# Splitting the softmax terms, placing the statistics' steps and reloading z in a dilated-attention kernel

## The chip, the cores and the metric

The kernel runs on one core of a Trainium2 chip. The metric is device microseconds of one execution. Five runs of the kernel before gave 5422.48 to 5433.66 us, with a median of 5424.08 us.

The engines are named as the profile names them: PE (TensorE) with PEld for its weight loads, DVE (VectorE), ACT (ScalarE), POOL (GpSimd) and SP (SyncE, whose queue issues nearly all DMAs).

## The reference

The input x is 16 images of 56 x 56 pixels and 384 channels, in float32. Two layers are computed, each of them a residual on a group norm with 32 groups of 12 channels:

```
x = x + attention(group_norm(x), w_qkv, w_proj, b_proj)
x = x + depthwise_conv3x3(group_norm(x), sign(clip(w, -1, 1)))
```

The attention is local. The 384 channels of q, k and v are three groups of 128 with dilations 1, 2 and 3, each of 4 heads of 32 channels. A pixel attends to its 9 neighbours in a 3 x 3 pattern with that dilation; outside the image k and v are zero:

```
scores  = sum over 32 channels of q[pixel] * k[neighbour], times 32 ** -0.5
weights = softmax over the 9 neighbours
out     = sum over 9 neighbours of weights * v[neighbour]
y       = out, three groups side by side, times w_proj, plus b_proj
```

The statistics of a group norm cover a whole image, so each layer of an image can start only when the layer before it has finished the image.

## The kernel before, in words

**Tiling.** An image is cut into 7 chunks of 8 rows (448 pixels), so there are 112 chunks. Channels lie on the partitions, pixels along the free dimension. Three stages run through the chunks in a software pipeline, all at the same time on different chunks:

- `plan_a` loads x, transposes it on PE (`turn`, L412), copies it out on ACT, collects statistics on DVE (L425), and writes it to DRAM as `xd`.
- `plan_b` is the attention. `load_x` and `normalise` prepare `xn`; `k_or_v` and `query` project it on PE (L463); `score` multiplies q by k on DVE (L516) and sums over channels on PE (L501); `softmax_1` to `softmax_3` make the weights; `turn_weights` (L566) transposes them with a DMA from SP into `aT`; `weigh` spreads them over the channels on PE (L579), multiplies by v on DVE (L586, into a buffer `w` of a pool of three) and adds on POOL (L594, L597, L598); `out_project` multiplies by w_proj on PE (L612), adds the residual on DVE (L615), collects statistics (L618) and writes `x1d` to DRAM (L620).
- `plan_c` is the convolution. Two thirds of the channels go through PE: `load` (L688) brings `z`, three shifted copies of the rows with 32 channels each, `normalise` scales it on ACT (L701) and sets edges to zero on POOL (L682, L703), `convolve` (L715) multiplies by diagonal matrices, and DVE adds the residual (L722). The last third (`xg`, L729, normalised into `zg` at L740) is scaled by its nine taps on ACT (L762) and added on POOL (L768, L773, L776). `turn` transposes the result back (L783), ACT copies it (L785), and it is written out (L788).

In the last image, where no attention runs any more beside the convolution, `plan_c` takes other ways: the nine taps of `xg` run on DVE (`taps_last`, L753), one z set of four is normalised on DVE (L697), outputs are issued from ACT, and z is loaded as `z_last` into pairs of sets in buffers that the attention has left (pool `t` for even chunks, pool `w` and one `xn` for odd ones). Each pair takes three transfers, one for each of the three rows of taps (`ky`).

**The softmax weights.** The weights are made in float32 (`ew`) and then written as three bfloat16 terms whose sum is the weight. ACT casts the first term (L558), POOL subtracts it (L559, into `rest`), ACT casts the second (L560), POOL subtracts again and so makes the third (L561). All four stand in `softmax_3`.

**The statistics.** `group_norm` makes six steps: `channels` aggregates on DVE (L305); `mean`, `deviation` and `variance` each sum over groups with small matmuls (L311, L321, L331); `invert` computes an inverse square root with 13 small instructions on POOL (L345 to L349); `spread_out` copies mean and scale back to the channels with small matmuls (L354 into `pp`, and L367 into `pz` for the convolution) and two copies on DVE (L358 `mr`, L372 `mrz`). For the input of the convolution all later work on an image (`zg`, `z`) needs `mr` or `mrz`.

**What sets the order.** The function `at(when, order, piece)` files each piece of work under a slice and an order inside the slice; a chunk advances by 9 slices (`STEP`). The pieces are issued sorted by slice and order. This is a priority, not yet the queue: when the program is built, a planner walks through a model of the machine and lets each engine take, of the instructions whose inputs and buffers it expects to be ready, the one of the highest priority. The result is one fixed queue for each engine, which the chip runs in order; an instruction that waits holds up all that stand behind it. DMAs stand in the queue of the engine that issues them. The orders of a slice are

```
SOFTMAX, SCORE, CONVOLVE, WEIGH, QUERY, STATISTICS, QKV, PROJECT, STAGE_A, STAGE_C, NORM, LOADS
```

The six steps of the statistics of `x1` are filed at slices 0, 1, 2, 4, 5 and 7 after the image's last `out_project` (`STAT1_SLICE`), those of x likewise (`STAT0_SLICE`), all of them with order `STATISTICS`.

Of the kernel before, what the change touches and what calls it, by code (L numbers as in the profile page):

```python
# [8 lines left out]
F32 = mybir.dt.float32  # L9
# [3 lines left out]
ALU = mybir.AluOpType  # L13
# [4 lines left out]
P = 128  # L18
HEADS = 4
HD = 32  # L20
NG = 3
NTAP = 9
NQ = 4
ROWS = 8
SUB = 112
# [3 lines left out]
NPAD = 32  # L29
K_SLOTS, V_SLOTS = 2, 3  # L30
RSQRT_BITS = 0x5F3759DF
TERMS = 3
# [3 lines left out]
def dilated_attention_then_binary_conv(  # L36
# [28 lines left out]
    nc = tc.nc  # L65
# [214 lines left out]
    def rows(ap):  # L280
        return ap.rearrange("p (r w) -> p r w", w=W)
# [100 lines left out]
    def at(when, order, piece):  # L382

        pieces.setdefault((when, order), []).append(piece)
# [6 lines left out]
    def plan_a(m, t0):  # L391
# [41 lines left out]
        def norm(k):  # L433
            if k == 0:
                steps["of"] = group_norm(stats0.pop(b), lambda mr: mr0.update({b: mr}))
            steps["of"][k]()
# [3 lines left out]
            at(t0 + 2 * j if b else FIRST + 2 * c + 1, STAGE_A, lambda j=j: turn(j))  # L440
        if c == NCH - 1:
            for k in range(6):
                at(t0 + 5 + STAT0_SLICE[k], STATISTICS, lambda k=k: norm(k))

    def plan_b(m, t0):

# [98 lines left out]
        def softmax_2():  # L545
# [2 lines left out]
            nc.vector.reciprocal(sm, sm)  # L548
            nc.vector.tensor_tensor(by_neighbour(weights), by_neighbour(weights), over_neighbours(sm), ALU.mult)

        def softmax_3():

            rest = s_p.tile([SUB, NSUB * NPAD * HEADS], F32, tag="rest", name="rest")
            eights = "p (u k) -> p u k"
            e8 = ew.rearrange(eights, k=8)
            r8 = rest.rearrange(eights, k=8)
            term = [e3.rearrange("p s u (r k) -> p (s u r) k", r=4)[:, :, 8 * t : 8 * t + 8] for t in range(TERMS)]
            nc.scalar.copy(term[0], e8)  # L558
            nc.gpsimd.tensor_tensor(r8, e8, term[0], ALU.subtract)  # L559
            nc.scalar.copy(term[1], r8)  # L560
            nc.gpsimd.tensor_tensor(term[2], r8, term[1], ALU.subtract)  # L561

# [61 lines left out]
        def norm(k):  # L624
            if k == 0:
                steps["of"] = group_norm(stats1.pop(b), lambda mr, mrz: mr1.update({b: (mr, mrz)}), True)
            steps["of"][k]()
# [10 lines left out]
        at(t0 + 9, SOFTMAX, softmax_1)  # L638
        at(t0 + 10, SOFTMAX, softmax_2)
        at(t0 + 11, SOFTMAX, softmax_3)  # L640
        at(t0 + 12, LOADS, turn_weights)
        for i in range(9):
            at(t0 + 14 + i, WEIGH, lambda i=i: weigh(i))
# [2 lines left out]
            at(t0 + 24 + j, PROJECT, lambda j=j: out_project(j))  # L646
        if c == NCH - 1:
            for k in range(6):
                at(t0 + 27 + STAT1_SLICE[k], STATISTICS, lambda k=k: norm(k))

    def plan_c(m, t0):

# [16 lines left out]
        def load(j):  # L669
            by_set = x1d[b].rearrange("(j q c) n -> j c q n", q=NQ, c=HD)[j]  # L670
            if b < B - 1:
                z = z_p.tile([P, NQ * PX], F32, tag="z", name="z")[:K3].rearrange("p (q n) -> p q n", q=NQ)
                had[f"z{j}"] = [(z, 0, NQ)]
            else:

                had[f"z{j}"] = []
                for q0 in range(0, NQ, 2):
                    pool, tag = (t_p, "t") if c % 2 == 0 else (w_p, "w") if (j, q0) != (1, 2) else (xn_p, "xn")
                    z = pool.tile([P, 3, PX], F32, tag=tag, name="z_last")[:K3, :2]
                    had[f"z{j}"].append((z, q0, q0 + 2))  # L680
            for edge in edges(j):
                nc.gpsimd.memset(edge, 0.0)  # L682
            for ky in range(3):
                lo = W if c == 0 and ky == 0 else 0
                hi = PX - W if c == NCH - 1 and ky == 2 else PX
                n0 = p0 + (ky - 1) * W
                for z, q0, q1 in had[f"z{j}"]:
                    nc.sync.dma_start(  # L688
                        z[ky * HD : (ky + 1) * HD, :, lo:hi], by_set[:, q0:q1, n0 + lo : n0 + hi]
                    )  # L690

        def normalise(j):
            mrz = mr1[b][1]
# [31 lines left out]
        zp = zg[m % 2]  # L725

        def load_g():
            had["xg"] = xg = xg_p.tile([P, ROWS + 2, W], F32, tag="xg", name="xg")
            nc.sync.dma_start(  # L729
                xg[:, lo:hi, :].rearrange("p r w -> p (r w)"),  # L730
                x1d[b][JG * P : (JG + 1) * P, p0 + (lo - 1) * W : p0 + (hi - 1) * W],
            )
# [57 lines left out]
        if b == B - 1:  # L790

            at(t0 - 6, LOADS, load_g)
            at(t0 - 6, LOADS, load_x)
            ahead = 3 if c else 1
            at(t0 - ahead, NORM, normalise_g)
            for j in range(JG):
                at(t0 - 5 + j, LOADS, lambda j=j: load(j))
                at(t0 - ahead + j, NORM, lambda j=j: normalise(j))
                at(t0 + 1 + j, CONVOLVE, lambda j=j: convolve(j))
            for ky in range(3):  # L800
                at(t0 + 1 + ky, CONVOLVE, lambda ky=ky: taps_last(ky))
            for s in range(NSUB):
                at(t0 + 12, STAGE_C, lambda s=s: turn(s))
            return
# [11 lines left out]
        for s in range(NSUB):  # L816
            at(t0 + 9 + s, STAGE_C, lambda s=s: turn(s))

    SOFTMAX, SCORE, CONVOLVE, WEIGH, QUERY, STATISTICS, QKV, PROJECT, STAGE_A, STAGE_C, NORM, LOADS = range(12)
    STEP = 9  # L820
    STAT0_SLICE = (0, 1, 2, 4, 5, 7)
    STAT1_SLICE = (0, 1, 2, 4, 5, 7)
    FIRST = -200
    at(FIRST, LOADS, load_weights)
    for cc in range(NG):
# [41 lines left out]
```

## Time and profile before

| what | value |
|---|---|
| median of 5 runs | 5424.08 us |
| the profiled execution's own time | 5424.08 us |
| its span, first to last instruction | 5422.4 us |
| granted clock of PE, mean | 0.978 |
| PE busy | 5206.4 us |
| POOL busy | 4219.4 us |
| DVE busy | 4141.3 us |
| ACT busy | 2401.1 us |
| HBM read and written | 466.41 MB and 231.21 MB |

Busy time is the union of an engine's instructions; a busy PE also contains time at half clock. A window of the profile lists, for each engine, the busy microseconds and the number of instructions in a stretch of the span, then the granted clock, the mean busy share of the 16 DMA engines, and GB/s. A list of waits names the engine and line that stood still, after the arrow what ended the wait, and then the total in us, the number of times and the longest. A line of the timeline has the start and the duration in us, the engine, the line of the kernel, the instruction, what it writes and reads, and in brackets how long the engine stood idle before it and what ended that. "SPq" is the DMA queue of SP.

The steady part of the program lasts from about 480 us to 4800 us. After 5262 us the attention is over and only the convolution of the last image is left.

### The profile page before, as it was taken

How to read it: one execution, taken by the hardware profiler on the slowest of the kernel's cores; microseconds unless marked ns; L12 is line 12 of the kernel's file. 1: busy time of each engine (PE TensorE's matmuls, PEld its weight loads, DVE VectorE, ACT ScalarE, POOL GpSimd, SP SyncE). 2: the span in 40 equal slices, each digit the busy share in tenths (PEclk: the TensorE clock that was granted, in tenths of full speed). 3: DMA queues.
4: the chain of work that ended last, by engine and by line, in shares of the span. 5: the costliest groups of instructions: out<-in, count | busy, mean ns of one | idle time of the engine just before them, and what ended most of it. 6: DMA issues, size and time to landing. Idle time of an engine off the chain costs nothing. (4 is left out here: it accounts for less than half of the span.)

```text
span 5422.4 us, 77496 instructions
## 1 busy us (share of the span) xinstructions
PE 5206.4 (96%) x27669; PEld 2427.8 (45%) x27669; DVE 4141.3 (76%) x4209; ACT 2401.1 (44%) x4189; POOL 4219.4 (78%) x3049
## 2 busy tenths in 40 slices
PE   8999999999999999999999999999999999999965
PEld 4444444444444444444444444444444444444422
DVE  4887778877777787777878777787777877777753
ACT  3224444445444444444445444444444445444433
POOL 2677888878888887888878888887888878888870
PEclk9999999999999999999999999999999999999976
DMA  5444555655556555555655555555555655544444
GB/s 167 126 119 125 160 158 150 161 158 161 154 157 165 163 156 161 159 157 150 165 156 161 155 156 164 162 156 162 158 157 151 166 155 162 152 136 132 129 122 129
DMA packets 811640, 825.75 MB, mean 152 GB/s; under 512 B 360307, under 2 KB 801014, under 8 KB 811254
## 3 DMA queue, kind: packets, MB, share of 16 engines
q1 hardware_dynamic: 803270, 808.79, 54.3%
q10 hardware_dynamic: 7984, 12.00, 0.7%
q8 instruction: 219, 3.59, 0.3%
q14 instruction: 167, 1.37, 0.1%
HBM read 466.41 MB, written 231.21 MB: 129 GB/s over the span
## 5 line engine op out<-in xcount | busy, mean ns | idle before, releaser
L594 POOL TENSOR_TENSOR w<-w 128x1344 f32<-128x1344 f32 x672 | 2050.6, 3051 | 459.8 <-DVE w L586 358.3
L586 DVE TENSOR_TENSOR w<-pb_a,v 128x1344 f32<-128x1344 f32 x1008 | 1560.6, 1548 | 249.5 <-PE pb_a L579 152.5
L516 DVE TENSOR_TENSOR t<-pq,k 128x1344 f32<-128x1344 f32 x1008 | 1535.3, 1551 | 245.9 <-PE pq L463 245.9
L463 PE MATMUL pkv<-xn,wqkvT 128*128 128x448 f32 x3924 | 1565.6, 548 | 0.0
L463 PEld LDWEIGHTS pkv<-xn,wqkvT 128*128 128x128 f32 x3924 | 717.3, 190 | 660.0 <-issue 629.8
L612 PE MATMUL po<-y,wprojT 128*128 128x448 f32 x2016 | 831.8, 549 | 22.4 <-POOL y L598 19.2
L768 POOL TENSOR_TENSOR m<-m 128x1344 f32<-128x1344 f32 x210 | 640.2, 3049 | 269.4 <-ACT m L762 269.4
L463 PE MATMUL pq<-xn,wqkvT 128*128 128x448 f32 x1962 | 826.7, 557 | 0.0
L701 ACT ACTIVATE z<-z,mrz 96x448 f32<-96x448 f32 x840 | 578.4, 751 | 437.9 <-DMA z<-x1d 411.2
L501 PE MATMUL ps<-t,sel 128*32 128x448 f32 x6048 | 676.9, 558 | 35.9 <-DVE t L516 35.3
L762 ACT ACTIVATE m<-zg,ktap 128x448 f32<-128x448 f32 x945 | 554.0, 658 | 285.6 <-POOL m L768 278.5
L612 PEld LDWEIGHTS po<-y,wprojT 128*128 128x128 f32 x2016 | 375.4, 191 | 375.6 <-issue 342.0
L715 PE MATMUL pc<-z,kdiag 96*32 96x440 f32 (+1 forms) x5040 | 523.0, 549 | 6.3 <-POOL z L703 4.4
L722 DVE TENSOR_TENSOR x<-pc,x 128x448 f32<-128x448 f32 x224 | 139.8, 624 | 457.5 <-PE pc L715 457.5
L463 PEld LDWEIGHTS pq<-xn,wqkvT 128*128 128x128 f32 x1962 | 345.2, 189 | 311.5 <-issue 311.5
L579 PE MATMUL pb_a<-aT,spread 24*128 24x448 bf16 x3024 | 368.7, 359 | 44.4 <-DVE w L586 39.0
L598 POOL TENSOR_TENSOR y<-y,w 128x448 f32<-128x448 f32 x336 | 381.8, 1136 | 22.6
L597 POOL TENSOR_TENSOR y<-w 128x448 f32<-128x448 f32 x336 | 382.4, 1138 | 14.7
L473 ACT COPY v<-pkv 128x448 f32<-128x448 f32 x336 | 178.8, 532 | 473.3 <-PE pkv L463 458.1
L615 DVE SCALAR_TENSOR_TENSOR xr<-po,bias,xr 128x448 f32<-128x448 f32 x336 | 227.7, 678 | 187.3 <-PE po L612 183.4
L473 ACT COPY k<-pkv 128x448 f32<-128x448 f32 x336 | 178.5, 531 | 369.5 <-PE pkv L463 369.5
L501 PEld LDWEIGHTS ps<-t,sel 128*32 128x32 f32 x6048 | 171.7, 110 | 378.7 <-issue 249.1
(128 smaller groups left out, 4406.3 us busy)
## 6 DMA issues: line engine op xcount, KB each, us to landing
z<-x1d SPq DMA_DIRECT2D x570, 224.0 KB, 4.1
xr<-xd SPq DMA_DIRECT2D x112, 672.0 KB, 4.3
x1d<-xr SPq DMA_DIRECT2D x112, 672.0 KB, 3.2
xn<-xd SPq DMA_DIRECT2D x109, 672.0 KB, 4.6
xin<-in_x_dram SPq DMA_DIRECT2D x108, 672.0 KB, 7.1
xd<-xa SPq DMA_DIRECT2D x315, 224.0 KB, 3.6
out_dram<-osb SPq DMA_DIRECT2D x420, 168.0 KB, 3.5
x<-x1d SPq DMA_DIRECT2D x112, 448.0 KB, 7.6
```

The lines of the kernel that those rows point to most:

```text
L463: nc.tensor.matmul(dst[:, :PX], wqkvT[:, cc, o0 : o0 + P], had["xn"][:, cc, :], start=(cc == 0), stop=(cc == NG - 1))
L501: return nc.tensor.matmul(had["ps"][32 * j : 32 * j + 32, :PX], sel[:, s0 : s0 + 32], tk, start=(issued[j] == 1), stop=(issued[j] == len(r ...
L516: nc.vector.tensor_tensor(t.rearrange("p k (r w) -> p k r w", w=W), q3, k3, ALU.mult)
L586: nc.vector.tensor_tensor(w.rearrange("p k (r w) -> p k r w", w=W), pb[:, :, :PX].rearrange("p k (r w) -> p k r w", w=W), three(kv[1][g][m ...
L594: nc.gpsimd.tensor_tensor(w0, w0, w, ALU.add)
L597: nc.gpsimd.tensor_tensor(y, w0[:, 0], w0[:, 1], ALU.add)
L598: nc.gpsimd.tensor_tensor(y, y, w0[:, 2], ALU.add)
L612: nc.tensor.matmul(po[:, :PX], wprojT[:, g, j * P : (j + 1) * P], had[f"y{g}"], start=(g == 0), stop=(g == NG - 1))
L701: nc.scalar.activation(z, z, AF.Identity, bias=mrz[:, j, q, 0:1], scale=mrz[:, j, q, 1:2])
L715: return nc.tensor.matmul(pcr[q * HD : (q + 1) * HD, :, lo:hi], kdiag[:, kx, j * NQ + q, :], rows(set_of(j, q))[:, :, lo + kx - 1 : hi + k ...
L762: nc.scalar.activation(rows(t[:, kx]), zp[:, ky : ky + ROWS, kx : kx + W], AF.Copy, scale=ktap[:, o : o + 1])
L768: nc.gpsimd.tensor_tensor(had["m"], had["m"], t, ALU.add)
```

## The change

- The second half of the three terms (cast L560, subtraction L561) becomes a piece of its own, `softmax_4`, one slice later than the first half. `turn_weights` stays in that later slice.
- `STATISTICS` moves ahead of `CONVOLVE`, `WEIGH` and `QUERY` in the order of a slice. Only `channels` and `invert`, the steps without matmuls, keep it (`STAT_ORDER`); the other four get the new order `SPREAD`, which stands where `STATISTICS` stood.
- `spread_out` of `x1` moves from slice 7 to slice 6.
- In chunks 1 to 5 of the last image z is loaded set by set: one transfer brings 96 partitions, that is three rows of taps by 32 channels, from an access pattern whose outermost dimension steps by one image row, three times. Chunks 0 and 6 keep the transfers by `ky`.
- In the last image `xg` moves from its pool of two to the pool of `xn` (three buffers), the odd chunks' fourth z pair moves from `xn` to `xr`, and `load_x` is filed three slices later, behind the loads of z.

```diff
--- before.py
+++ after.py
@@ -440,7 +440,7 @@
             at(t0 + 2 * j if b else FIRST + 2 * c + 1, STAGE_A, lambda j=j: turn(j))
         if c == NCH - 1:
             for k in range(6):
-                at(t0 + 5 + STAT0_SLICE[k], STATISTICS, lambda k=k: norm(k))
+                at(t0 + 5 + STAT0_SLICE[k], STAT_ORDER[k], lambda k=k: norm(k))
 
     def plan_b(m, t0):
 
@@ -548,15 +548,18 @@
             nc.vector.reciprocal(sm, sm)
             nc.vector.tensor_tensor(by_neighbour(weights), by_neighbour(weights), over_neighbours(sm), ALU.mult)
 
+        EIGHTS = "p (u k) -> p u k"
+        e8 = ew.rearrange(EIGHTS, k=8)
+        term = [e3.rearrange("p s u (r k) -> p (s u r) k", r=4)[:, :, 8 * t : 8 * t + 8] for t in range(TERMS)]
+
         def softmax_3():
 
-            rest = s_p.tile([SUB, NSUB * NPAD * HEADS], F32, tag="rest", name="rest")
-            eights = "p (u k) -> p u k"
-            e8 = ew.rearrange(eights, k=8)
-            r8 = rest.rearrange(eights, k=8)
-            term = [e3.rearrange("p s u (r k) -> p (s u r) k", r=4)[:, :, 8 * t : 8 * t + 8] for t in range(TERMS)]
+            had["rest"] = rest = s_p.tile([SUB, NSUB * NPAD * HEADS], F32, tag="rest", name="rest")
             nc.scalar.copy(term[0], e8)
-            nc.gpsimd.tensor_tensor(r8, e8, term[0], ALU.subtract)
+            nc.gpsimd.tensor_tensor(rest.rearrange(EIGHTS, k=8), e8, term[0], ALU.subtract)
+
+        def softmax_4():
+            r8 = had["rest"].rearrange(EIGHTS, k=8)
             nc.scalar.copy(term[1], r8)
             nc.gpsimd.tensor_tensor(term[2], r8, term[1], ALU.subtract)
 
@@ -638,6 +641,7 @@
         at(t0 + 9, SOFTMAX, softmax_1)
         at(t0 + 10, SOFTMAX, softmax_2)
         at(t0 + 11, SOFTMAX, softmax_3)
+        at(t0 + 12, SOFTMAX, softmax_4)
         at(t0 + 12, LOADS, turn_weights)
         for i in range(9):
             at(t0 + 14 + i, WEIGH, lambda i=i: weigh(i))
@@ -646,7 +650,7 @@
             at(t0 + 24 + j, PROJECT, lambda j=j: out_project(j))
         if c == NCH - 1:
             for k in range(6):
-                at(t0 + 27 + STAT1_SLICE[k], STATISTICS, lambda k=k: norm(k))
+                at(t0 + 27 + STAT1_SLICE[k], STAT_ORDER[k], lambda k=k: norm(k))
 
     def plan_c(m, t0):
 
@@ -675,7 +679,7 @@
 
                 had[f"z{j}"] = []
                 for q0 in range(0, NQ, 2):
-                    pool, tag = (t_p, "t") if c % 2 == 0 else (w_p, "w") if (j, q0) != (1, 2) else (xn_p, "xn")
+                    pool, tag = (t_p, "t") if c % 2 == 0 else (w_p, "w") if (j, q0) != (1, 2) else (xr_p, "xr")
                     z = pool.tile([P, 3, PX], F32, tag=tag, name="z_last")[:K3, :2]
                     had[f"z{j}"].append((z, q0, q0 + 2))
             for edge in edges(j):
@@ -685,9 +689,17 @@
                 hi = PX - W if c == NCH - 1 and ky == 2 else PX
                 n0 = p0 + (ky - 1) * W
                 for z, q0, q1 in had[f"z{j}"]:
+                    if b == B - 1 and 0 < c < NCH - 1:
+                        continue
                     nc.sync.dma_start(
                         z[ky * HD : (ky + 1) * HD, :, lo:hi], by_set[:, q0:q1, n0 + lo : n0 + hi]
                     )
+            if b == B - 1 and 0 < c < NCH - 1:
+
+                for q in range(NQ):
+                    one = by_set[:, q, p0 - W : p0 - W + PX]
+                    three_rows = bass.AP(one.tensor, one.offset, [(W, 3), *one.ap])
+                    nc.sync.dma_start(set_of(j, q), three_rows)
 
         def normalise(j):
             mrz = mr1[b][1]
@@ -725,7 +737,11 @@
         zp = zg[m % 2]
 
         def load_g():
-            had["xg"] = xg = xg_p.tile([P, ROWS + 2, W], F32, tag="xg", name="xg")
+            if b < B - 1:
+                had["xg"] = xg = xg_p.tile([P, ROWS + 2, W], F32, tag="xg", name="xg")
+            else:
+                xg = xn_p.tile([P, NG, PX], F32, tag="xn", name="xg_last").rearrange("p j n -> p (j n)")
+                had["xg"] = xg = rows(xg[:, : (ROWS + 2) * W])
             nc.sync.dma_start(
                 xg[:, lo:hi, :].rearrange("p r w -> p (r w)"),
                 x1d[b][JG * P : (JG + 1) * P, p0 + (lo - 1) * W : p0 + (hi - 1) * W],
@@ -790,7 +806,7 @@
         if b == B - 1:
 
             at(t0 - 6, LOADS, load_g)
-            at(t0 - 6, LOADS, load_x)
+            at(t0 - 3, LOADS, load_x)
             ahead = 3 if c else 1
             at(t0 - ahead, NORM, normalise_g)
             for j in range(JG):
@@ -816,10 +832,12 @@
         for s in range(NSUB):
             at(t0 + 9 + s, STAGE_C, lambda s=s: turn(s))
 
-    SOFTMAX, SCORE, CONVOLVE, WEIGH, QUERY, STATISTICS, QKV, PROJECT, STAGE_A, STAGE_C, NORM, LOADS = range(12)
+    SOFTMAX, SCORE, STATISTICS, CONVOLVE, WEIGH, QUERY, SPREAD, QKV, PROJECT, STAGE_A, STAGE_C, NORM, LOADS = range(13)
+
+    STAT_ORDER = (STATISTICS, SPREAD, SPREAD, SPREAD, STATISTICS, SPREAD)
     STEP = 9
     STAT0_SLICE = (0, 1, 2, 4, 5, 7)
-    STAT1_SLICE = (0, 1, 2, 4, 5, 7)
+    STAT1_SLICE = (0, 1, 2, 4, 5, 6)
     FIRST = -200
     at(FIRST, LOADS, load_weights)
     for cc in range(NG):
```

## The prediction

> **What bounds the kernel now.** I read the page first, then the busy time of each engine stretch by stretch, then what PE waited for, then the order of time around one of its waits, and last the SP queue at the end of the program.
>
> The page: busy shares, and the slices of the span.
>
> ```profile
> PE 5206.4 (96%) x27669; PEld 2427.8 (45%) x27669; DVE 4141.3 (76%) x4209; ACT 2401.1 (44%) x4189; POOL 4219.4 (78%) x3049
> PE   8999999999999999999999999999999999999965
> PEclk9999999999999999999999999999999999999976
> ```
>
> Windows (stretch, its length, busy us of each engine with counts, granted clock, DMA share, GB/s):
>
> ```profile
> 480.00:4800.00 4320.00, 4255.28 (x22902) 1983.22 (x22902) 3388.14 (x3415) 2014.97 (x3517) 3533.65 (x2459) 0.99 0.58 158
> 5286.00:5423.00 137.00, 75.50 (x429) 38.14 (x421) 53.69 (x86) 45.22 (x75) 2.00 (x11) 0.65 0.44 129
> 2435.00:2440.00 5.00, 3.31 (x20) 0.99 (x24) 3.63 (x4) 2.21 (x5) 4.30 (x2) 0.56 1.04 322
> 2440.00:2445.00 5.00, 5.00 (x31) 1.58 (x24) 1.47 (x2) 4.39 (x8) 3.56 (x3) 0.76 0.86 213
> ```
>
> PE is the bound: from 480 to 4800 us it is idle 65 us of 4320. Only at the end, from 5286, is it idle 61 of 137. A gain must come from these two places; the 44% of ACT or the 78% of POOL are no gain by themselves. The waits of PE from 480 to 4800 (total us, times, longest):
>
> ```profile
> PE ps L501 <- DVE t L516: 26.9, 15, 2.0
> PE pb_a L579 <- DVE w L586: 24.6, 15, 7.1
> PE pv L331 <- POOL dev L325: 11.2, 14, 0.9
> PE pt_o L783 <- ACT k L473: 4.4, 13, 0.3
> ```
>
> The first two come as a pair, once per image, 14 times. In order of time around 2400 us:
>
> ```profile
> 2393.37 0.36 PE L579 MATMUL pb_a<-aT,spread 24*128 24x448 bf16 x3
> 2393.66 4.78 PE L463 MATMUL pkv<-xn,wqkvT 128*128 128x448 f32 x12
> 2395.45 0.18 POOL L347 TENSOR_SCALAR var<-var 32x1 f32<-32x1 f32 x1
> 2395.58 0.28 POOL L682 MEMSET z<- 32x224 f32 x1
> 2396.09 0.18 POOL L349 TENSOR_TENSOR pair<-pair 32x1 f32<-32x1 f32 x1
> 2400.83 0.72 PE L354 MATMUL pp<-pair,gselT 32*128 32x2 f32 x6
> 2403.51 0.81 ACT L740 ACTIVATE zg<-xg,mr 128x504 f32<-128x504 f32 x1 [4.50 <-DVE mr L358]
> 2432.15 1.56 DVE L586 TENSOR_TENSOR w<-pb_a,v 128x1344 f32<-128x1344 f32 x1 [3.17 <-POOL w L594]
> 2433.76 0.37 PE L579 MATMUL pb_a<-aT,spread 24*128 24x448 bf16 x3 [1.33 <-DVE w L586]
> 2436.69 3.21 PE L501 MATMUL ps<-t,sel 128*32 128x448 f32 x16 [2.03 <-DVE t L516]
> ```
>
> The statistics of x1 reach ACT at 2403.51, 4.50 us late. The first chunk's convolution of that image then runs late on ACT and POOL, POOL falls behind with the additions of L594, the buffer of w is not free, DVE waits 3.17 and PE 1.33 + 2.03. The clock falls after it (0.56 and 0.76 in two windows of 5 us: 2.2 + 1.2 = 3.4 us lost there). The windows of 100 us that hold such a place show 0.97 or 0.98, so 2 to 3 us each; 2.3 x 14 = 32 us in all.
>
> At the end, SP's waits from 5290 to 5400, and a load burst with the quiet after it:
>
> ```profile
> SPq L729 <- PE pt_o L783: 49.4, 6, 11.4
> 5317.00:5327.00 10.00, 3.94 (x24) 1.99 (x24) 5.66 (x9) 5.84 (x9) 0.00 (x0) 0.66 0.92 282
> 5327.00:5334.80 7.80, 6.19 (x42) 3.17 (x36) 2.42 (x5) 0.86 (x2) 0.00 (x0) 0.78 0.01 2
> ```
>
> SP stands at the load of xg until the chunk two before has been turned (49.4 us in six waits), with all loads of z behind it. Loads and matmuls take turns: 10 us at 0.92 of the DMA engines, then 8 us at 0.01. The first matmuls of chunks 1 to 6 start from 5307.70 to 5393.50: 17.2 us a chunk.
>
> **The change, part by part.** The sum is made against the profiled execution: span 5422.4, own time 5424.08, which is also the median.
>
> *Softmax terms in two slices.* The same two casts (0.62 us) and two subtractions (1.16 us) per chunk; nothing is added. The second pair and the transposing load behind it on SP may come later by whatever enters between: one addition of L594 is 3.05 us. What hides it: in the chunk at 2472 us the second subtraction ends at 2477.73, the transposed weights land at 2481.78, the first matmul on them is at 2488.26, so 6.5 us are spare. ACT no longer stands at L560 (252.6 us over the run), but PE waits for ACT only 4.4 + 2.3 us. In three of the last five chunks the spare time is gone (landed 5169.27, first matmul 5169.31): 0 to 3 x 3.05 = 9 us. I take 2, since POOL there often has nothing ready to put in between.
>
> *Statistics first in their slices.* The three aggregations on DVE (0.34 each) and the 13 small POOL instructions (2390.84 to 2396.27) are moved past additions of the same slice. In the trace the 13 already stand before that slice's L594 (2396.58), and the mean's matmuls keep their place: 0. If they did push one L594 back, 3.4 us on POOL, still before the slack of DVE (2.3 us idle around 2390) is gone: at most 1 us an image, 14 in all, or as much gained.
>
> *spread_out of x1 one slice earlier.* This is where the stall goes. The new place of pp is behind pb_a of the slice before, at 2393.66, ahead of pkv. Its input, pair, is ready at 2396.27. Will the planner that writes the queues know this? It puts an instruction where it expects the inputs. The memset of the next z buffer waits for convolution matmuls that end at 2390.62 (SP's load into that buffer goes at 2390.75), yet in POOL's order it stands behind the eleventh of the 13. So the planner expects the eleventh at about 2390.7; on the chip it ran at 2395.45. It will think pair ready by about 2391 and put pp at 2393.66. PE, whose queue is in order, then waits 2.6 us, with pkv, po and the k and v copies on ACT behind it: 14 x 2.6 = +36.5. The bounds: 0 if pp lands behind pkv, 3.8 (one of the 13 later, and latency) above; I take 2.6, worked out from this place itself. In return mr comes some 6 us earlier (pp takes 0.72, pz 0.68), while what follows on PE moves 2.6 later, so ACT and POOL gain over 8 us on it against the 3.17 that DVE lacked: the pair 26.9 + 24.6 and the 4.4 for pt_o go, -55.9. The wait for dev (11.2) stays. For the clock, one wait of 2.6 against two of 3.4 together: ends 0 and -32, I take -16, for no row shows a lone wait of this size. Sum: -35.4.
>
> The Trainium skill ("TensorE: Matmul & The Clock Gate", Part 1) says that the clock is halved after an idle window of about 3.4 us. By that rule a wait of 2.6 never fills a window, and 16 us more would go; but here two waits of 1.33 and 2.03 with matmuls between them did cost the clock.
>
> *The last image's loads.* Chunks 1 to 5 load z in 8 transfers of 168 KB in place of 12 of 112 KB; xg has a third buffer and x comes after z, so SP's 49.4 us of waiting ahead of z goes. Were only this so, the chunk would fall from 17.2 to what is next: PE 2 x 4.9 + 1.7 = 11.5 at the low clock, ACT 7.3 busy and 2.4 waiting for output buffers, DMA 9.2 at full share. That is 12, five chunks: -26. But each new transfer reads 3 overlapping rows, and its outermost count is 3. The trace has one load with three outer rows, that of the bias at 2.31 us: its semaphore has one event at 3.26 and then three, at 15.79, 15.96 and 16.60, where the loads beside it, of 112 rows, have sixteen. I take it that the new loads run on three DMA engines of the sixteen. Price: 40 x 168 KB = 6.88 MB, 2.29 MB an engine. An engine moves 282 / 0.92 / 16 = 19 GB/s in the burst above; in the quietest loads, 672 KB in 4.1 against 224 KB in 3.0 us, 26 GB/s. So 88 to 119 us, and 24 to 32 for the engine's share of x, xg, outputs and chunk 6: 112 to 151. Today the same stretch, from 5291.0 to the last landing at 5397.3, is 106. So +6 to +45, and 13 less if the first loads go at once after chunk 0's (5277.7). With the end of the sixteen engines the bounds are -26 and +45; I take +16, nearer to the quiet row, since thirteen engines would be mostly idle.
>
> The Trainium skill ("DMA: Bandwidth & Descriptors", "Why a DMA increments its semaphore by 16 and not by 1") states the rule: the engines used are the largest number up to 16 that divides the slowest dimension of both sides, here 3 and 96, so 3; its "Rules for kernel authors" warn of an outermost dimension under 16. It speaks against this part of the change: by it the tail loses 16, by the look of the other loads of z it gains 26.
>
> Sum: 2 + 0 - 35.4 + 16 = -17.4; 5424.1 - 17.4 = 5407.
>
> **Rivals.**
> B, no wait at pp: the planner puts it behind pkv, or POOL is earlier. For it: the first subtraction and the additions may shift POOL. Against: the memset's place. -55.9 - 32 + 18 = -70: 5354.
> C, slower: the wait at pp comes and the old stall stays, because the planner also moves POOL's L768 of the first chunk ahead by as much as mr, and ACT is as late for it as now (POOL waits 2.31 and 1.74 for ACT there). +36.5 + 18 = +54: 5479. It decides as soon as less than 18.5 of the 55.9 goes.
> D, the z loads run on all engines after all (the destination has 96 rows): the tail takes turns no more. -35.4 - 26 + 2 = -59: 5365.
>
> **How the numbers follow.** A, as summed: 0.46; B 0.16; C 0.26; D 0.12. A's own range, by clock and tail, is 5375 to 5435. A change of 0.2% (10.8 us, so 5413 and 5435) is about what can be told from none here. A gives 0.30 faster, 0.12 same, 0.04 slower; B and D are faster, C slower: 0.58, 0.12, 0.30. The range from 5345 to 5470 leaves out C's upper half and a little of B.
>
> **What would show it.** Right: pp directly behind pb_a with a wait of 2 to 3 us on POOL pair, some 14 times; zg not waiting for mr; no DVE wait of 3 us at L594; z_last of chunks 1 to 5 landing 2 to 3 us after each other at a DMA share near 0.2 to 0.3; SP no longer at xg for pt_o. Wrong: a DMA share of 0.9 in the tail (D), no idle PE before pp (B), DVE still waiting for L594 in the first chunk (C). A steady chunk that shows new PE waits for aT would break the 6.5 us of cover, and the whole sum.

## The result and the profile after

The changed kernel takes 5441.59 us (median), the kernel before takes 5430.0 us on the same chips: a ratio of 1.0023, with a 95% interval of 1.0018 to 1.0028. The forecast was 5407, so a gain of 0.3%; it is a loss of 0.23%. The profiled execution after has a span of 5442.0 us (before: 5422.4).

The page of the changed kernel: busy shares, the granted clock in 40 slices, and the chain that ended last.

```profile
PE 5231.8 (96%) x27669; PEld 2428.3 (45%) x27669; DVE 4147.3 (76%) x4209; ACT 2409.0 (44%) x4189; POOL 4212.7 (77%) x3049
...
PEclk9999999999999999999999999999999999999976
...
DMA 2%; PE 0%; SPq 0%; ACT 0%; issue 0%; DVE 0%; ACTq 0%; POOL 0%; DVEq 0%; POOLq 0%
```

PE is still the bound, and its counts are the same. The chain that ended last holds 2% of the span in DMA, all of it loads of z_last; before it was 1% PE and 0% DMA. To place the 19.6 us between the two spans I take the last pv of the run, which stands at 5270.93 before and at 5275.76 after: 4.8 us are lost ahead of it, 14.8 behind it.

What PE waited for from 480 to 4800 us (total, times, longest):

```profile
PE pp L354 <- POOL pair L349: 34.1, 13, 2.9
PE pv L331 <- POOL dev L325: 10.9, 13, 0.9
PE pb_a L582 <- DVE w L589: 5.1, 2, 4.9
PE po L615 <- ACT k L473: 4.7, 5, 1.6
PE ps L501 <- DVE t L516: 0.3, 1, 0.3
```

The pair that was 26.9 + 24.6 is gone from every image but the first, and the wait of pp for pair has come in its place, once per image. All waits in these rows add up to 55.1 us, where those of before add up to 69.4. DVE's waits for the additions of POOL, which the forecast named as the cause of the old pair, fall from 44.2 to 3.0 us in this part. In order of time around one such place, and the clock in two windows of 5 us right behind it:

```profile
2402.41 3.06 POOL L597 TENSOR_TENSOR w<-w 128x1344 f32<-128x1344 f32 x1 [2.04 <-DVE var L334]
...
2407.96 0.36 PE L582 MATMUL pb_a<-aT,spread 24*128 24x448 bf16 x3
...
2410.69 0.18 POOL L349 TENSOR_TENSOR pair<-pair 32x1 f32<-32x1 f32 x1
...
2410.93 0.82 PE L354 MATMUL pp<-pair,gselT 32*128 32x2 f32 x6 [2.61 <-POOL pair L349]
...
2411.99 0.81 ACT L756 ACTIVATE zg<-xg,mr 128x504 f32<-128x504 f32 x1 [10.02 <-DVE mr L358]
```

```profile
2410.00:2415.00 5.00, 4.07 (x58) 2.64 (x59) 2.89 (x4) 0.81 (x1) 3.78 (x5) 0.76 0.26 56
2415.00:2420.00 5.00, 5.00 (x15) 2.21 (x14) 3.02 (x2) 3.20 (x6) 1.39 (x1) 0.90 0.25 65
```

PE stands behind pb_a for 2.61 us, as in the forecast's own size, and then runs at 0.76 and 0.90: the 3.4 us at half clock that used to follow the pair follow the single wait as well. From 500 to 4800 us the trace of before has 13 stretches at half clock, 58.0 us in all, which cost 29.0 us of full-speed work; the trace after has 14, also 58.0 us. One trace could have shown this by chance, but over the four profiles of this study in which PE has the order of before in this part, 25.6 to 32.4 us are lost, and over the four in which it has that of the changed kernel, 25.6 to 29.0. The window of the whole part shows the same clock as before, 0.99:

```profile
480.00:4800.00 4320.00, 4264.65 (x22900) 1991.04 (x22902) 3398.53 (x3417) 2022.77 (x3518) 3528.18 (x2456) 0.99 0.58 158
```

The first image's boundary, which the forecast counted like any other (waits of PE from 400 to 510 us, first the longest one before, then all after):

```profile
PE pb_a L579 <- DVE w L586: 7.3, 2, 7.1
```

```profile
PE pp L354 <- POOL pair L349: 5.2, 1, 5.2
PE pb_a L582 <- DVE w L589: 5.1, 2, 4.9
PE ps L501 <- DVE t L516: 2.9, 1, 2.9
```

Before, there was one wait of 7.1 us and 6.8 us at half clock; after, there are these three, and 20.5 us at half clock (3.4 against 10.2 us lost). Why pp waits longer here stands in the order of time, before and after:

```profile
443.01 0.18 POOL L349 TENSOR_TENSOR pair<-pair 32x1 f32<-32x1 f32 x1
445.13 0.72 PE L354 MATMUL pp<-pair,gselT 32*128 32x2 f32 x6
```

```profile
442.92 0.18 POOL L349 TENSOR_TENSOR pair<-pair 32x1 f32<-32x1 f32 x1
443.16 1.44 PE L354 MATMUL pp<-pair,gselT 32*128 32x2 f32 x6 [5.17 <-POOL pair L349]
```

The change brings PE to pp 7.1 us earlier (437.99 in place of 445.13), as it does in the later images (2393.66 in place of 2400.83 in the forecast). But before, pair was ready 1.9 us ahead of pp here, and 4.6 us ahead there; so the wait is 5.2 us here and 2.6 there. Seen from the matmuls of the variance, the changed kernel is level with the one before up to this place (0.1 us ahead), 12.3 us late at the next ones and 4.8 us late at the last: behind the first image it gained 7.5 us in all.

The tail. The stretch from 5290 to 5380 us in one window, before and after (PE busy, weight loads, DVE, ACT, POOL, clock, DMA share, GB/s), then, after, what PE waited for from 5300 to 5420 and the issues of the new loads on SP (shortest, median, longest issue in ns):

```profile
5290.00:5380.00 90.00, 48.58 (x271) 24.66 (x270) 36.40 (x59) 32.53 (x53) 1.26 (x7) 0.65 0.50 144
5290.00:5380.00 90.00, 50.92 (x261) 17.18 (x261) 32.08 (x54) 28.09 (x45) 0.73 (x4) 0.63 0.35 117
```

```profile
PE pc L727 <- DVE z_last L709: 45.3, 9, 8.5
```

```profile
L702 SPq DMA_DIRECT2D z_last<-x1d x40: 685/1199/4289, 5290.4 to 5390.2; - x40
```

PE waits for normalised z, which waits for the loads, while the DMA engines are busy for 0.35 of the time (before: 0.50, with bursts of 0.92). Each of the 40 transfers shows on its semaphore (the counter that tells of its end) one event early and three together at its end: the second one at 5296.82 and then at 5300.61, 5300.64 and 5300.77. The ends of successive transfers are 2.1 to 2.9 us apart while the queue is full (5300.77, 5303.04, 5305.31, 5307.58, 5310.46, 5312.52). From the first matmul of chunk 1 to that of chunk 5 a chunk took 18.1 us before (5307.70 to 5380.19 in four); here it takes 22.3 (5305.99 to 5395.02 in four).

### The profile page after: what moved, and what is told of

Same layout as the page of the kernel before. It is cut to its first block, busy times and chain, and to the rows that moved or that the text cites. A ratio compares the mean times of both kernels' runs of the same rounds, so it can differ in the third digit from the quotient of the medians.

```text
span 5442.0 us, 77423 instructions
## 1 busy us (share of the span) xinstructions
PE 5231.8 (96%) x27669; PEld 2428.3 (45%) x27669; DVE 4147.3 (76%) x4209; ACT 2409.0 (44%) x4189; POOL 4212.7 (77%) x3049
## 5 line engine op out<-in xcount | busy, mean ns | idle before, releaser
L463 PE MATMUL pkv<-xn,wqkvT 128*128 128x448 f32 x3924 | 1596.8, 556 | 0.0
L501 PE MATMUL ps<-t,sel 128*32 128x448 f32 x6048 | 663.4, 548 | 9.8 <-DVE t L516 9.1
L424 ACT COPY xa<-pt_x 128x448 f32<-128x448 f32 x315 | 168.2, 534 | 377.7 <-PE pt_x L412 374.6
```

What stands on the lines that cost most here:

```text
L463: nc.tensor.matmul(dst[:, :PX], wqkvT[:, cc, o0 : o0 + P], had["xn"][:, cc, :], start=(cc == 0), stop=(cc == NG - 1))
L501: return nc.tensor.matmul(had["ps"][32 * j : 32 * j + 32, :PX], sel[:, s0 : s0 + 32], tk, start=(issued[j] == 1), stop=(issued[j] == len(r ...
```

## The experiments

Every ratio is to the kernel before, measured in alternation on the same chip.

### The parts alone: loads, slice, softmax

**tail_only** is the kernel before with the last image's loads alone:

```diff
+                    if b == B - 1 and 0 < c < NCH - 1:
+                        continue
...
+            if b == B - 1 and 0 < c < NCH - 1:
+                for q in range(NQ):
+                    one = by_set[:, q, p0 - W : p0 - W + PX]
+                    three_rows = bass.AP(one.tensor, one.offset, [(W, 3), *one.ap])
+                    nc.sync.dma_start(set_of(j, q), three_rows)
...
+                xg = xn_p.tile([P, NG, PX], F32, tag="xn", name="xg_last").rearrange("p j n -> p (j n)")
...
-            at(t0 - 6, LOADS, load_x)
+            at(t0 - 3, LOADS, load_x)
```

> The kernel before with the last image's loads of the change alone: z of chunks 1 to 5 by sets, three rows of image in one transfer; xg in a third buffer; x after z. Theory (the transfers whose outermost count is 3 run on three DMA engines, 168 KB in 2.25 us one after the other): the tail grows by the 16 us that the two profiles differ by behind the last image's pv, so +16 (+10 to +20); the 40 transfers end with one event and then three, about 2.3 us apart. Rival (the tail loses for another reason that came with the statistics or the softmax): 0 or a gain, to -26.

Measured: 5441.15 us against 5427.14, ratio 1.0027 (1.0018 to 1.0036): +14.0. From the last pv to the end it takes 167.0 us, against 151.5 before and 166.2 in the changed kernel. The theory's range was +10 to +20. So the loads alone cost as much as the whole change does, and the rival, no loss, is out.

**slice6_only** is one number:

```diff
-    STAT1_SLICE = (0, 1, 2, 4, 5, 7)
+    STAT1_SLICE = (0, 1, 2, 4, 5, 6)
```

> The kernel before with the last step of the x1 statistics in slice 6 in place of 7, and nothing else. Theory: this alone is the whole of what changed ahead of the tail: a wait of pp for pair of about 2.6 us once per image takes the place of the pair of 1.3 and 2.0, and the boundary of the first image is late by some 12 us more; +3.6 in sum (0 to +8). Rival 1 (the first image's loss belongs to the softmax in two slices): -9. Rival 2 (the forecast's, without the clock): -19.

Measured: 5425.25 against 5427.14, ratio 0.9996 (0.9987 to 1.0004): -1.9 us (-7 to +2), no change. Its waits of PE from 480 to 4800 us:

```profile
PE pp L354 <- POOL pair L349: 33.9, 13, 2.9
PE pv L331 <- POOL dev L325: 11.1, 14, 0.9
PE pb_a L579 <- DVE w L586: 3.6, 1, 3.6
PE po L612 <- ACT k L473: 3.3, 6, 0.8
```

The sums are those of the changed kernel, and the waits at the first image are there too (5.1, 2.9 and 3.6 us): both the exchange of waits and the first image's loss belong to this one number. Both rivals, -9 and -19, lie outside the interval; the theory's +3.6 lies just above it, and only the lower end of its range, 0 to +2, agrees.

**split_only** has the softmax's terms in two slices and nothing else:

```diff
...
             nc.scalar.copy(term[0], e8)
-            nc.gpsimd.tensor_tensor(r8, e8, term[0], ALU.subtract)
+            nc.gpsimd.tensor_tensor(rest.rearrange(EIGHTS, k=8), e8, term[0], ALU.subtract)
+
+        def softmax_4():
+            r8 = had["rest"].rearrange(EIGHTS, k=8)
             nc.scalar.copy(term[1], r8)
...
+        at(t0 + 12, SOFTMAX, softmax_4)
```

> The kernel before with the softmax terms in two slices and nothing else. Theory: nothing at all moves, for the planner gives every engine and every queue the same order of instructions as before: 0 (-5 to +5, what two measurements of one kernel differ by), the groups of casts and subtractions as before (0.62 and 1.16 us each), the second subtraction of the chunk at about 2472 us directly behind the first. Rival (the forecast's term): additions of 3.05 us come in between in some chunks, +2 to +9.

Measured: 5430.03 against 5427.96, ratio 1.0008 (0.9999 to 1.0017): no change that can be told. The two traces have the same instructions in the same order on PE, DVE, ACT, POOL and SP: the planner had set the second pair where the new slice asks for it. So the rival, that additions come in between, is out by the order, though its +2 to +9 is not by the time. The same comparison of the kernel before with by_ky_slice7 (below) shows what the statistics' new places in their slices do without the change of slice: ahead of the last image's tail they move 15 instructions on DVE, the aggregations into ch, and none elsewhere.

### The shape of the transfers

**by_ky** is the changed kernel with z loaded by rows of the window again, and the buffer of xg and the place of x as changed:

```diff
-                    if b == B - 1 and 0 < c < NCH - 1:
-                        continue
...
-                for q in range(NQ):
-                    ...
-                    nc.sync.dma_start(set_of(j, q), three_rows)
```

> The changed kernel with z of the last image loaded by rows of the kernel window again (12 transfers of 112 KB a chunk, outermost count 32), xg still in a third buffer and x still after z. Theory (three engines): the loads leave all 16 engines, SP does not stand at xg, and the chunk falls from 17.2 us to about 12: -26 against before in the tail, +4 ahead of it, so -22 (-30 to -12). Rival (the order of the loads or the buffers are what costs): still +12 to +20.

Measured: 5398.94 against 5427.14, ratio 0.9949 (0.9935 to 0.9962): -28. The stretch from 5290 to 5380 us:

```profile
5290.00:5380.00 90.00, 60.04 (x393) 33.08 (x391) 47.19 (x77) 38.80 (x65) 1.94 (x9) 0.73 0.61 177
```

A share of 0.61 in place of 0.35, 177 GB/s in place of 117, 393 matmuls done in place of 261. The chunk takes 13.5 us (five from 5303.18 to 5370.80), where the forecast's rival D had estimated 12. From the last pv to the end it takes 122.0 us, where the kernel before takes 151.5 and the changed one 166.2. So the third buffer for xg and the later x together are worth some 30 us, and the transfers by sets gave back all of it and 15 more.

**by_ky_slice7** goes back to slice 7 as well:

```diff
-    STAT1_SLICE = (0, 1, 2, 4, 5, 6)
+    STAT1_SLICE = (0, 1, 2, 4, 5, 7)
```

> As the one before it, and the last step of the x1 statistics back in slice 7; the softmax stays in two slices. Theory: the tail's gain alone, -26 (-34 to -16), with the old waits of PE once per image (1.3 and 2.0 us) as before, since the softmax in two slices moves no time. Rival (the softmax in two slices costs some us per image): 10 us worse than by_ky.

Measured: 5393.36 against 5427.14, ratio 0.9938 (0.9926 to 0.9951): -34, at the lower end of what the theory gave. The rival, 10 us more than by_ky, is out. Its interval overlaps that of by_ky, which agrees with slice6_only.

**z24_by_set** keeps the order by sets and takes only the shape away:

```diff
-                    three_rows = bass.AP(one.tensor, one.offset, [(W, 3), *one.ap])
-                    nc.sync.dma_start(set_of(j, q), three_rows)
+                    for ky in range(3):
+                        n0 = p0 + (ky - 1) * W
+                        nc.sync.dma_start(set_of(j, q)[ky * HD : (ky + 1) * HD], by_set[:, q, n0 : n0 + PX])
```

> The changed kernel with each set of the last image loaded in three transfers of 32 rows and 56 KB in place of one transfer of three times 32 rows and 168 KB: the same sets in the same order, 24 transfers a chunk. Tells the shape of a transfer from the order by sets. Theory (three engines because the outermost count is 3): the transfers leave all engines, each ends with 16 events; the tail loses at most SP's 24 issues a chunk (0.4 to 0.6 us each, 10 to 14 us a chunk) and stays near by_ky's: ratio to before 0.994 to 0.999. Rival (loading by sets costs, whatever the shape): as the changed kernel, 1.002 or more.

Measured: 5400.02 against 5422.3, ratio 0.9959 (0.9942 to 0.9975): inside the theory's range, with the same sets in the same order, in 24 transfers a chunk in place of 8. Its issues on SP (ns), and the same stretch:

```profile
L702 SPq DMA_DIRECT2D z_last<-x1d x120: 302/419/1077, 5278.5 to 5363.5; - x120
```

```profile
5290.00:5380.00 90.00, 59.99 (x325) 37.51 (x326) 44.12 (x71) 39.03 (x62) 1.98 (x9) 0.65 0.61 173
```

These transfers of 56 KB end with sixteen events each, in the five timed here all within 0.4 us, and follow each other as SP issues them, 0.46 us apart (last events at 5300.46, 5300.97, 5301.30, 5301.89, 5302.38): 168 KB in 1.4 us instead of 2.26. From the last pv to the end it takes 133.0 us: 33.2 of the 44.2 us between the changed kernel and by_ky come back when only the shape of the transfers changes, and with it their number. So it is mainly the three in front of the pattern that costs. The 11.0 us that by_ky is still ahead belong to the order by sets or to the 24 issues in place of 12, which no run separates.

The Trainium skill ("DMA: Bandwidth & Descriptors", "Why a DMA increments its semaphore by 16 and not by 1") says that the engines used are the largest number up to 16 that divides the slowest dimension of both sides, and that the sequencer writes the other increments at once. The runs agree: one early event and three late ones for 3 against 96, sixteen for 32 against 32.

### What the wait of pp costs, and the clock

**pp_behind_pkv** is by_ky with the last step of the statistics in the same slice, but behind the k and v matmuls:

```diff
-    SOFTMAX, SCORE, STATISTICS, CONVOLVE, WEIGH, QUERY, SPREAD, QKV, PROJECT, STAGE_A, STAGE_C, NORM, LOADS = range(13)
+    SOFTMAX, SCORE, STATISTICS, CONVOLVE, WEIGH, QUERY, SPREAD, QKV, PP, PROJECT, STAGE_A, STAGE_C, NORM, LOADS = range(14)
-    STAT_ORDER = (STATISTICS, SPREAD, SPREAD, SPREAD, STATISTICS, SPREAD)
+    STAT_ORDER = (STATISTICS, SPREAD, SPREAD, SPREAD, STATISTICS, PP)
```

> by_ky with the last step of the x1 statistics still in slice 6, but put behind the k and v matmuls of its slice (4.8 us later on PE). Tells what the wait of 2.6 costs, and what the clock has to do with it. Theory: pair is ready, the wait of pp goes (-2.6 x 13), mr comes some 1.8 us later than in by_ky and still 3 us earlier than in the kernel before, so at most 1.5 us of the old pair of waits returns; and with no wait of PE over 1 us at the boundary there is no stretch of 3.4 us at half clock (-1.7 x 13): -30 to -55 against by_ky. Rival 1 (the clock falls at the boundary whatever PE waits for): no more than -2.6 x 13 = -34, with the half-clock stretches still there. Rival 2 (the old pair of waits returns whole): by_ky +5, as by_ky_slice7 with its order.

Measured: 5353.67 against 5427.96, ratio 0.9863 (0.9849 to 0.9876), 45 us below by_ky, inside the theory's 30 to 55. The order of time at one boundary, the waits from 480 to 4800, and that stretch in one window:

```profile
2377.09 4.78 PE L463 MATMUL pkv<-xn,wqkvT 128*128 128x448 f32 x12
...
2379.51 0.18 POOL L349 TENSOR_TENSOR pair<-pair 32x1 f32<-32x1 f32 x1
...
2381.80 0.83 PE L354 MATMUL pp<-pair,gselT 32*128 32x2 f32 x6
...
2382.96 0.81 ACT L748 ACTIVATE zg<-xg,mr 128x504 f32<-128x504 f32 x1 [0.52 <-DVE mr L358]
```

```profile
PE po L615 <- ACT k L473: 13.0, 13, 2.3
PE pb_a L582 <- DVE w L589: 12.9, 14, 1.9
PE pv L331 <- POOL dev L325: 11.0, 13, 0.9
PE ps L501 <- DVE t L516: 1.7, 5, 0.5
```

```profile
480.00:4800.00 4320.00, 4281.25 (x23128) 1999.24 (x23126) 3456.49 (x3444) 2044.44 (x3553) 3560.05 (x2484) 1.00 0.58 160
```

pair is ready 2.1 us before PE comes to pp, and ACT waits 0.52 for mr where it waited 10.02. Of the old pair, 0.84 us per image is back. Against by_ky the waits in this stretch fall from 52.0 to 38.6 us, and the work lost at half clock falls from 32.4 to 3.4: the clock makes 29.0 of the gain and the waits 13.4. Rival 1 (a clock that falls whatever PE waits for) is out, and so is rival 2.

All 13 profiles of this study together show when the clock falls. Counted from 500 to 4800 us, single waits of PE of over 0.4 us with none other within 4 us, and the stretch at half clock that begins at most 4 us after each:

```
wait of PE, us   times   no half clock   3.4 us   6.8 us   more
0.4 to 1.0        232        232            0        0       0
1.0 to 1.5         15         13            2        0       0
1.5 to 2.0         11          5            6        0       0
2.0 to 3.0         54          0           44       10       0
3.0 to 3.5         24          0            0       24       0
5.0 to 5.1         26          0            0       22       4
1.3 and 2.0        52          1           34       17       0   (two waits, 0.9 us of matmuls between)
```

No stretch at half clock in that part of the runs begins anywhere else.

**late_pp_only** is the statistics of pp_behind_pkv in the kernel before, with its loads and its softmax:

```diff
...
+    SOFTMAX, SCORE, STATISTICS, CONVOLVE, WEIGH, QUERY, SPREAD, QKV, PP, PROJECT, STAGE_A, STAGE_C, NORM, LOADS = range(14)
+
+    STAT_ORDER = (STATISTICS, SPREAD, SPREAD, SPREAD, STATISTICS, PP)
...
-    STAT1_SLICE = (0, 1, 2, 4, 5, 7)
+    STAT1_SLICE = (0, 1, 2, 4, 5, 6)
```

> The kernel before with the statistics' order and slice of the change, and the last step behind the k and v matmuls; loads and softmax as before. Theory (tail and statistics add up): 5354 - 5399 + 5425 = 5380, so -47 against before (-55 to -38). Rival (part of pp_behind_pkv's gain came with the tail): -30 or less.

Measured: 5380.63 against 5422.3, ratio 0.9916 (0.9899 to 0.9932): -42, inside the range given; the rival's -30 is out. Tail and statistics add up within this error. Its two largest waits of PE from 480 to 4800 us, where all of them add up to 39.6:

```profile
PE pb_a L579 <- DVE w L586: 13.0, 14, 1.8
PE po L612 <- ACT k L473: 12.6, 13, 1.9
```

**late_pp_later_pv** is pp_behind_pkv with the variance's matmul behind the four transposes (the lines against pp_behind_pkv):

```diff
-    SOFTMAX, SCORE, STATISTICS, CONVOLVE, WEIGH, QUERY, SPREAD, QKV, PP, PROJECT, STAGE_A, STAGE_C, NORM, LOADS = range(14)
+    SOFTMAX, SCORE, STATISTICS, CONVOLVE, WEIGH, QUERY, SPREAD, QKV, PP, PROJECT, STAGE_A, PV, STAGE_C, NORM, LOADS = range(15)
...
-    STAT_ORDER = (STATISTICS, SPREAD, SPREAD, SPREAD, STATISTICS, PP)
+    STAT_ORDER = (STATISTICS, SPREAD, SPREAD, PV, STATISTICS, PP)
```

> pp_behind_pkv with the variance's matmul behind the four transposes of its slice (0.6 us later), to take away its wait for dev (0.87 us, 13 times). In GpSimd's order the subtraction of 1.16 us and one addition of 3.05 us now stand among the 13 instructions that lead to pair. Theory: pair comes some 4 us later, pp waits 1.5 to 3 us again, and the clock falls with it as in by_ky: +20 to +40 against pp_behind_pkv. Rival (dev's wait goes and pair is still in time): -5 to -12.

Measured: 5344.25 against 5422.3, ratio 0.9853 (0.9837 to 0.9869): the lowest time of the study, 9 us below pp_behind_pkv where the theory had it 20 to 40 above. The rival was right. From 480 to 4800 us pp waits once, and the waits for dev have left the list:

```profile
PE pb_a L582 <- DVE w L589: 12.8, 14, 1.8
PE po L615 <- ACT k L473: 11.2, 12, 1.8
PE ps L501 <- DVE t L516: 3.1, 8, 0.6
PE pp L354 <- POOL pair L349: 0.2, 1, 0.2
```

The place in GpSimd's order on which the theory stood is that of the statistics of x, not of x1. There pair comes at 2501.56 in place of 2499.31, but pp comes no earlier than 2505.91. At x1's boundary pair is ready at 2377.78 and pp starts at 2379.77. The two kernels were timed in different sets of runs; the ratios overlap (0.9849 to 0.9876 against 0.9837 to 0.9869), so of the 9 us only the waits for dev (11.0 to none) are shown.

### Another way to have pair in time

**invert_on_dve** is by_ky with the 13 small instructions on VectorE (12 of the three rounds, and the product):

```diff
-                nc.gpsimd.tensor_tensor(t, r, r, ALU.mult)
+                nc.vector.tensor_tensor(t, r, r, ALU.mult)
...
-            nc.gpsimd.tensor_tensor(pair[:, 0:1], pair[:, 2:3], pair[:, 1:2], ALU.mult)
+            nc.vector.tensor_tensor(pair[:, 0:1], pair[:, 2:3], pair[:, 1:2], ALU.mult)
```

> by_ky with the 13 small instructions that lead to pair on VectorE in place of GpSimd. Theory (pp waits because these 13 stand behind an addition of 3.05 us and between two of 1.13 us in GpSimd's queue): pair is ready before pp, the wait of 2.6 goes, mr is earlier still, and GpSimd has 13 x 0.27 us less: -30 to -60 against by_ky. Rival (VectorE's queue holds them up as well, behind w and t of 1.55 us each): the wait stays at 1 to 4 us, within 10 us of by_ky.

Measured: 5553.34 against 5427.96, ratio 1.0231 (1.0217 to 1.0245): 154 us above by_ky. Neither the theory nor its rival had this. pp waits no more, but two waits of pb_a in each image came in its place. From 480 to 4800 us, and one boundary in order of time:

```profile
PE pb_a L582 <- DVE w L589: 105.6, 26, 5.1
```

```profile
2467.50 3.06 POOL L597 TENSOR_TENSOR w<-w 128x1344 f32<-128x1344 f32 x1 [2.04 <-DVE var L334]
...
2468.21 2.36 DVE L345 TENSOR_TENSOR var<-var 32x1 f32<-32x1 f32 x1
...
2470.64 1.13 POOL L600 TENSOR_TENSOR y<-w 128x448 f32<-128x448 f32 x1
2470.78 0.14 DVE L347 TENSOR_SCALAR var<-var 32x1 f32<-32x1 f32 x1
2470.96 0.81 DVE L348 TENSOR_TENSOR var<-var 32x1 f32<-32x1 f32 x1
...
2471.84 1.13 POOL L601 TENSOR_TENSOR y<-y,w 128x448 f32<-128x448 f32 x1
2471.99 0.99 DVE L346 TENSOR_TENSOR var<-var 32x1 f32<-32x1 f32 x1
...
2476.29 0.37 PE L582 MATMUL pb_a<-aT,spread 24*128 24x448 bf16 x3 [3.18 <-DVE w L589]
```

Products of 32x1, which in this trace take 0.15 us when no addition is running as they start, take 2.36, 0.81 and 0.99, and each ends with the addition on GpSimd that runs beside it: 2468.21 + 2.36 = 2470.57 and 2467.50 + 3.06 = 2470.56; 2471.77 and 2471.77; 2472.98 and 2472.97. The same holds for all 94 products of this chain that take over 0.3 us in the run: each ends within 0.02 us of the end of a GpSimd instruction. The instruction with one tensor (L347) takes 0.14 in all cases (0.12 to 0.14). VectorE's queue stands meanwhile, and with it w, which PE waits for twice per image, 5.06 us at the statistics of x and 3.18 at those of x1. Against by_ky the rows give +100.7 for this wait, -33.9 for pp, and the clock +59.8 (92.2 against 32.4): 127 of the 154 us; the rest is not assigned.

The Trainium skill ("SBUF — State Buffer", "SBUF: two separate sides") states a lock for it: VectorE and GpSimd share a pair of ports, and an operation of VectorE with two inputs in SBUF waits until a GpSimd operation that reads SBUF has ended. The ends above agree with that to 0.01 us.

**dev_invert_on_dve** moves the two small instructions of dev as well:

```diff
-            nc.gpsimd.tensor_tensor(dev, dev, dev, ALU.mult)
-            nc.gpsimd.tensor_tensor(dev, dev, ch[:, :, 1], ALU.add)
+            nc.vector.tensor_tensor(dev, dev, dev, ALU.mult)
+            nc.vector.tensor_tensor(dev, dev, ch[:, :, 1], ALU.add)
```

> As the one before it, with the two small instructions of dev on VectorE too. Theory: the wait of pv for dev (0.87 us, 13 times) goes as well: a further -5 to -12. Rival: the wait moves on to pv's next input or to VectorE's queue: 0.

Measured: 5541.14 against 5427.96, ratio 1.0209 (1.0195 to 1.0223): 12 below the one before it, at the end of the theory's range. The wait for dev (10.5 us there) is gone from the list, as the theory said, and the rival's 0 is out: the slowest of its four runs took 5544.82, the fastest of the other four 5550.18.

## Why the prediction was wrong

**The mechanism at pp was right to its size.** PE waits for pair 2.6 us once per image behind pb_a, the old pair and the wait of pt_o go, the wait for dev stays. The waits were to change by 36.5 - 55.9 = -19.4; from 480 to 4800 us they changed by -14.3 (69.4 to 55.1).

**The step that failed first is "ends 0 and -32, I take -16" for the clock.** It measured 0: 29.0 us lost before, 29.0 after. The forecast took a middle value for a wait of a size that no row showed. In the runs every one of the 54 single waits between 2.0 and 3.0 us brought a stretch at half clock, and none of the 232 below 1.0 us did. The upper end was the right one. The Trainium skill ("TensorE: Matmul & The Clock Gate", Part 1) speaks of an idle window of about 3.4 us; here 2.6 us of idle time is enough, and even 1.2 to 1.9 is sometimes, so a wait need not fill such a window. As in the prediction, the row had spoken against the page, and it was the row that held.

**The second is "14 x 2.6".** The first image is not like the others: pair leads pp by 1.9 us there in the kernel before, not by 4.6, so pp waits 5.2 us and ps 2.9 follows, +8.1 ahead of 480 us, and 6.8 us more are lost to the clock. The rows of before show this (443.01 and 445.13), but no row of that place had been read. Together: the waits gave -14.3 + 8.1 = -6.2 where -19.4 stood, and the clock +6.8 where -16 stood. So the statistics, -35.4 in the forecast, gained nothing: +0.6 by these sums, -1.9 (-7 to +2) in slice6_only.

**The tail's term held:** +16 forecast, +14.0 alone and +14.8 between the profiles. One event and then three, as for the bias, speak for three engines, and 168 KB in 2.26 us is then 25 GB/s an engine, next to the 26 of the quiet loads toward which the price was taken. The mechanism was right; that 16 came so close is partly luck, for it was a choice between -26 and +45. Rival D's size held for the other side: by_ky gains 28 in all, 26 had been given for loads on sixteen engines.

**The softmax's 2 us cannot be told from nothing** (+2, between -1 and +9 by its interval), and no instruction moved that could cost them; the statistics' places were taken at 0 and move only 15 instructions of DVE.

With -6.2, +6.8, 0 and +14.8 the sum is +15.4; the profiles differ by 19.6, the medians by 11.6. Most of these 8 us are the choice of the execution: the profiled one of before ran 5.9 us below its median, that of after 2.5 above. By the experiments on the parts, which do not depend on that choice, the sum is 14.0 - 1.9 + 2.1 = +14.2.

Rival C had the direction, but for another reason: the old stall did not stay. (Nor does its turning point, 18.5 of the 55.9, follow from its own terms: 36.5 + 18 are balanced by 54.5.) Rival B's condition, no wait at pp, is late_pp_only's, and there the statistics gain 42, half of the 88 that B counted (-55.9 - 32). The rows show why it is less: 0.84 to 0.86 us of the old pair comes back in each image and a wait of po for k with it (2.3 to 12.6 us), so the waits fall by 29.8 (69.4 to 39.6) and not by 55.9; the clock gives 27.2 (32.3 to 5.1). That these 57 us became 42 is not assigned.

Of the signs given ahead, pp behind pb_a, no DVE wait of 3 us for POOL's additions from 480 to 4800 us, the z loads 2 to 3 us apart and SP free of the wait at xg came true; the DMA share was 0.35 and not 0.2 to 0.3. That zg would not wait for mr is wrong: ACT stood 10.02 us for it, since zg had moved ahead in ACT's queue too. What this wait costs, if anything, no run shows.

## What to carry to other kernels

Where PE is the bound and its queue is in order, ask of each moved matmul not only whether its input is late but by how much: in these runs a wait of up to 1 us cost itself, one of 2 to 3 us brought 3.4 or 6.8 us at half clock with it, so 1.7 or 3.4 us of work more. Moving the same matmuls behind 4.8 us of work that needs nothing turned no gain (slice6_only) into 0.8% (late_pp_only).

Before several transfers are made into one, read the outermost count of the new pattern on both sides: 8 transfers of 168 KB with a 3 in front were slower than 24 of 56 KB with a 32.

A chain of small operations on VectorE is no cheap place beside long additions on GpSimd: with two inputs in SBUF (the chip's on-chip memory) a link of it waited here for up to a whole addition.

## What the runs showed of the hardware that was not expected

- The new transfers also hold their issuer. When none or few are under way an issue on SP takes about 0.7 us; behind several others most take longer (of the 40, 17 take 2.05 to 4.29 us; the row above: 685 ns shortest, 1199 median, 4289 longest), and the loads of x and xg among them take up to 2.33 us. In z24_by_set, with sixteen events a transfer, the median is 419 ns.
- VectorE's L345, L346 and L348 (the last in the first two of its three rounds) have means of 534, 922 and 721 ns in invert_on_dve, where the same operations on GpSimd had 204, 211 and 189 in the kernel before.
- The stretches at half clock come in steps: 3.4 us after a wait of 2.0 to 3.0 in 44 of 54 cases, 6.8 after one of 3.0 to 3.5 in all 24.
